# Relative products cut from eight to four at a place, value products to one block at a place, and the fourth unit's maxima folded earlier, in a two-layer attention kernel

## The chip, the cores and the metric

The kernel runs on one NeuronCore of a Trainium2 chip. The metric is the device time of one execution in microseconds (us). Three executions of the kernel before took 2415.1, 2431.35 and 2431.19 us; the median is 2431.19 us.

Names used here: PE is the matrix engine (TensorE), DVE the vector engine, ACT the scalar engine, POOL the GpSimd engine, and SP the sync engine, which here only issues transfers. PSUM is the memory that PE writes its products to.

## The reference

Eight images of 32 x 32 positions and 256 channels go through two layers. The first layer is a 3 x 3 convolution beside an attention of eight heads with relative position terms; the second is a plain attention and an expert network. What the change touches is the first layer's attention, cut here to its core:

```
kqv = einsum('bhwc,co->bhwo', x, qkv_w) + qkv_b           # k, q, v: 64 channels each
logits = einsum('bnid,bnjd->bnij', qf, kf)                # 1024 x 1024 for each head
rel_w = rel_logits_1d(qh, key_rel_w, H, W, ...)           # einsum of q with 63 relative keys,
rel_h = rel_logits_1d(qh_t, key_rel_h, W, H, ...)         # shifted to absolute positions
weights = softmax(logits + rel_w + rel_h, axis=-1)
attn = einsum('bnij,bnjd->bnid', weights, vf)
```

## The kernel before, in words

**Units and places.** The eight heads of an image form two groups of four (NG = 2), and the queries of a group form two halves of 512. A group and a half make a *unit*, so an image has four units. The tile `F` of a unit holds the query side of its logits on the partitions: the query itself, the two relative terms, and minus the row maximum. `KM` holds the key side. The logits of a unit are then single products of `KM` and `F`.

`first_layer(b)` walks over the four units of image `b`. Each unit has 32 *places* (eight key blocks times four heads), so an image has 128. At a place:

- `weigh` makes one product `st` (PE) and its exponential into `PT` (ACT);
- `score` makes products `lg` (PE) for the *next* unit and reduces each to a row maximum `mx` (DVE, line 782). A unit has 32 of them. The list `starts` says how many must be made by a given place;
- every fourth place `gather` multiplies `PT` with the values (`po`);
- when all 32 maxima stand, `fold` (place 25) combines them on DVE, `fold_in` (place 26) transposes them on PE (`pmx`) and copies them to `mb`, and `fold_out` (place 28) sends `mb` into the next unit's `F` by four small transfers issued on ACT (`F<-mb`, line 809);
- `fill.send` ends the place. It first runs what was put off to this place (`fill.later`), then lets the running chain go on to its next `yield None`, and then issues products of the convolution (`pc`) as far as the place's allowance of PE time is not used up.

After the first unit of an image, the whole second layer of the image before is worked off in one stretch of some 52 us.

**The chain of the next image.** `normalise(b + 1)` runs as such a chain during image `b`. From the first place of the third unit on it does, one step at a place: `queries` (transfers of the queries, lines 586 to 595), `values` (four blocks of products `pvv`, one block a place), three empty places, and then `features`. `features` makes the relative products: 32 for the columns and 32 for the rows, each a 128 x 64 product `prel`. A `piece` is eight of them in one PSUM tile of the pool that the `lg` tiles use too (four buffers). Four columns at four places, three rows at three places, two more places, the fourth row, three more places. A column's result goes through two copies on ACT (line 675) and two subtractions on DVE (line 676) into a float32r pair; a row's through one of each (lines 653 and 656). The subtractions run one place later, and a row's store into `fys` (line 661) one place after that. The four column stores into `fds` (line 682, 2 MB) follow the third row's stores in SP's queue.

Then `Unit(b + 1, 0)` is made. It issues six loads of its `F` on SP (lines 757 and 760, 2 MB). The buffer of this `F` is the one from which the rows are stored, so its first load waits until the last row store has landed. During the fourth unit of image `b` the maxima of this `Unit(b + 1, 0)` are made; the first `lg` product (place 5) needs the first three loads.

`combine(b + 1)` follows: four DVE operations, and, once the convolution of image `b` is done, ten more (line 534) at one a place.

**What sets the order.** The places write each engine's instructions in the order of the Python code; every engine works them off in that order. Transfers wait on SP, or on ACT, in the order of their issue.

Of the kernel before, what the change touches and what calls it, by code (L numbers as in the profile page):

```python
# [25 lines left out]
NG = NH // HG  # L26
# [12 lines left out]
def kernel(  # L39
# [72 lines left out]
    with ExitStack() as ph:  # L112
# [298 lines left out]
        def normalise(b):  # L411


            st = work.tile([P, KC, 2, 6], FP, tag="lst", name="gst")
            mv = work.tile([P, KC, 2], FP, tag="lmv", name="gmv")

            def turned(kc, g):
                tp = lg_tile("tpx")
                for k in range(4):
                    te.transpose(tp[:, k:512:4], T[b][g][:, k, kc * P : (kc + 1) * P], ident)  # L420
                return tp

# [24 lines left out]
            base = [b_tile("base") for kc in range(KC)]  # L447
            for g in range(2):
                for kc in range(KC):
                    nc.vector.tensor_scalar(  # L450
                        base[kc][:, g * 512 : g * 512 + 512],
                        turned(kc, g),
                        gm[:, kc, :],
                        gr[:, kc : kc + 1],
                        ALU.subtract,
                        ALU.mult,
                    )
                    yield None
            kq = b_tile("kq")
            kqh = work.tile([P, 2, S], FR, tag="kqh", name="kqh")  # L460
            kqb_ = kqh.bitcast(FP)

            for q in range(2):
                pk = lg_tile("pk")
                for kc in range(KC):
                    te.matmul(
                        pk,
                        lhsT=qkvw[:, kc, 0 : 2 * DK],
                        rhs=base[kc][:, 512 * q : 512 * (q + 1)],
                        start=kc == 0,  # L470
                        stop=kc == KC - 1,
                    )
                c = slice(q * 512, (q + 1) * 512)
                nc.scalar.activation(kq[:, c], pk, AF.Identity, bias=kqb, scale=kqs)
                nc.scalar.copy(kqh[:, 0, c], kq[:, c])
                nc.gpsimd.tensor_tensor(kqh[:, 1, c], kq[:, c], kqh[:, 0, c], ALU.subtract)
                yield None
            ready[b] = kqb_
            yield None
            while b > 0 and not may_query.get(b):  # L480
                yield None
            yield from queries(b)
            qs, qx, scr = spread.pop(b)
            if b > 0:
                keys(b, 0)
            for g in range(2):
                nc.gpsimd.tensor_tensor(T[b][g], T[b][g], l0b.to_broadcast([P, 4, C]), ALU.add)
            if b > 0:
                yield from values(b, base)
                for _ in range(3):  # L490
                    yield None
            yield from features(b, qs, qx, scr)
            units[b, 0] = Unit(b, 0)
            if b == 0:
                for g in range(NG):
                    keys(b, g, nc.scalar)
                yield None
                yield from values(b, base)
            while b > 0 and (done[b - 1] < 5 or not may_combine.get(b)):
                yield None  # L500
            yield from combine(b, base)
# [4 lines left out]
        def values(b, base):  # L506
            v0[b] = work.tile([P, NT, DK], FP, tag="v0", name="v0")
            for g in range(4):
                pv = lg_tile("pvv")[:, 0 : 2 * DK].rearrange("p (j c) -> p j c", c=DK)
                for j in range(2):  # L510
                    for kc in range(KC):
                        te.matmul(
                            pv[:, j, :],
                            lhsT=base[kc][:, (2 * g + j) * P : (2 * g + j + 1) * P],
                            rhs=qkvw[:, kc, 2 * DK : 3 * DK],
                            start=kc == 0,
                            stop=kc == KC - 1,
                        )
                nc.vector.tensor_tensor(
                    v0[b][:, 2 * g : 2 * g + 2], pv, vb.unsqueeze(1).to_broadcast([P, 2, DK]), ALU.add  # L520
                )
                yield None
# [104 lines left out]
        def features(b, qs, qx, scr):  # L627


            def piece(tab, src, q):  # L630
                pr = lg_tile("prel").rearrange("p (i g s) -> p i g s", g=NG, s=32)
                for n in range(8):
                    i = q * 8 + n
                    te.matmul(
                        pr[:, n],
                        lhsT=tab[:, (WW - 1 - i) * HG : (2 * WW - 1 - i) * HG],
                        rhs=src[:, :, i * 32 : (i + 1) * 32],
                        start=True,
                        stop=True,
                    )  # L640
                return pr
# [4 lines left out]
            ]  # L646

            def row(q):
                pr = piece(bhs, qs, q).rearrange("p i g s -> p g i s")
                r = b_tile("rel", FR) if q == 2 else scr[:, (2 + q % 2) * S : (3 + q % 2) * S]  # L650
                r = r.rearrange("p (l g s) -> p l g s", l=2, g=NG)
                hi, lo = (r[:, l].rearrange("p g (i s) -> p g i s", s=32) for l in range(2))
                nc.scalar.copy(hi, pr)

                def rest():
                    nc.vector.tensor_tensor(lo, pr, hi, ALU.subtract)
                    return store

                def store():
                    for g in range(NG):  # L660
# [2 lines left out]
                            in_=r.bitcast(FP)[:, :, g],  # L663
                        )

                fill.later(rest)

            def column(q):
                pr = piece(bws, qx, q)
                for g in range(NG):  # L670
                    ps = pr[:, :, g].rearrange("p x y -> p y x")
                    hi, lo = (
                        whole[g][:, l].rearrange("p (y x) -> p y x", x=WW)[:, :, q * 8 : q * 8 + 8] for l in range(2)
                    )
                    nc.scalar.copy(hi, ps)
                    fill.later(lambda ps=ps, hi=hi, lo=lo: nc.vector.tensor_tensor(lo, ps, hi, ALU.subtract) and None)
# [4 lines left out]
                    for p in (slice(HG, 64), slice(64, P)):  # L681
                        queue.dma_start(out=dst[p], in_=whole[g].bitcast(FP)[p])

            for q in range(4):
                column(q)
                yield None
            for q in range(3):
                row(q)
                yield None
                if b == 0 and q == 0:  # L690
                    store_columns(nc.scalar)
            yield None
            if b > 0:
                store_columns()
            yield None
            row(3)
            for _ in range(3):
                yield None

        done = {}  # L700
# [279 lines left out]
        def first_layer(b):  # L980


            more, sec = b + 1 < B, None
            starts = [lambda p: p * 4 // 3 + 1] * 3 + [lambda p: (p - 5) * 8 // 5 + 1]
            for s in range(NU * NT):
                n, j = divmod(s, NT)
                unit = units[b, n]
# [30 lines left out]
                for p in range(HG):  # L1018
                    place = 4 * j + p
                    unit.weigh(j, p)  # L1020
                    if nxt in units:
                        u = units[nxt]
                        while u.scored < min(32, starts[n](place)):
                            u.score()
                        if place == 25:
                            u.fold()
                        elif place == 26:
                            u.fold_in()
                        elif place == 28:
                            u.fold_out()  # L1030
                    elif nxt is not None:
                        assert place < 24
                    if p == 1:
                        if j > 0:
                            unit.gather()
# [489 lines left out]
```

## Time and profile before

The profiled execution took 2426.65 us; its span, from the first to the last instruction, is 2424.9 us.

| what | us |
|---|---|
| PE busy | 2203.9 (91% of the span) |
| DVE busy | 1384.1 (57%) |
| ACT busy | 1041.5 (43%) |
| POOL busy | 516.6 (21%) |
| `mx` reductions, 1024 | 657.8 |
| exponentials `PT`, 1024 | 596.9 |
| `st` products, 1024 | 519.2 |
| mean granted TensorE clock | 0.954 |

The first `st` runs at 124 us, the first layers end at 1858 us, and the expert network takes the rest. A table of the seven images in which the chain of the next image runs, from the trace's order of time (us from the start of the span; "third unit" is its first place, "column stores" the first issue of line 682, "F load" the first issue of line 757 after it, "first maximum product" the first `lg` of the next image, "next image" its first place):

| image | third unit | column stores | F load | first maximum product | next image |
|---|---|---|---|---|---|
| 0 | 204.2 | 230.7 | 243.5 | 251.5 | 282.4 |
| 1 | 422.1 | 450.0 | 462.2 | 478.6 | 509.8 |
| 2 | 654.8 | 681.8 | 694.3 | 703.0 | 733.6 |
| 3 | 875.1 | 907.2 | 920.1 | 930.9 | 961.4 |
| 4 | 1104.6 | 1138.6 | 1151.1 | 1163.3 | 1197.2 |
| 5 | 1338.8 | 1370.5 | 1383.8 | 1398.5 | 1429.0 |
| 6 | 1571.9 | 1605.7 | 1618.1 | 1630.7 | 1661.1 |

How to read it: the third unit takes 41 to 53 us although it holds the same work each time; and the last two columns are 30.4 to 33.9 us apart in every row.

### The profile page before, as it was taken

How to read it: one execution, taken by the hardware profiler on the slowest of the kernel's cores; microseconds unless marked ns; L12 is line 12 of the kernel's file. 1: busy time of each engine (PE TensorE's matmuls, PEld its weight loads, DVE VectorE, ACT ScalarE, POOL GpSimd, SP SyncE). 2: the span in 40 equal slices, each digit the busy share in tenths (PEclk: the TensorE clock that was granted, in tenths of full speed). 3: DMA queues.
4: the chain of work that ended last, by engine and by line, in shares of the span. 5: the costliest groups of instructions: out<-in, count | busy, mean ns of one | idle time of the engine just before them, and what ended most of it. 6: DMA issues, size and time to landing. Idle time of an engine off the chain costs nothing.

```text
span 2424.9 us, 28815 instructions
## 1 busy us (share of the span) xinstructions
PE 2203.9 (91%) x10515; PEld 1419.0 (59%) x10515; DVE 1384.1 (57%) x3147; ACT 1041.5 (43%) x1990; POOL 516.6 (21%) x446
## 2 busy tenths in 40 slices
PE   5589999899999999999899999999998789999998
PEld 4455556556555665566556556665664456666665
DVE  4667746575685666575657575657571633333333
ACT  2145544444454445444544454445454322222332
POOL 2213211320223022202120311131111042222220
PEclk7699999999999989998999899989998889999999
DMA  4634312701461245124312521361110121222210
GB/s 122 125 88 122 80 40 71 186 11 45 101 152 24 65 108 120 36 70 121 80 36 70 149 52 45 73 166 24 45 45 1 57 87 70 70 70 71 83 46 27
DMA packets 91935, 184.94 MB, mean 76 GB/s; under 512 B 9313, under 2 KB 37866, under 8 KB 90258
## 3 DMA queue, kind: packets, MB, share of 16 engines
q1 hardware_dynamic: 89426, 178.47, 29.2%
q10 hardware_dynamic: 2368, 4.63, 0.8%
q8 instruction: 84, 1.38, 0.2%
q14 instruction: 57, 0.47, 0.1%
HBM read 112.15 MB, written 62.52 MB: 72 GB/s over the span
## 4 chain that ended last, share of the span: by engine, by line
PE 64%; DVE 17%; DMA 7%; ACT 6%; SPq 3%; issue 2%; ACTq 1%; POOL 1%; DVEq 0%; POOLq 0%
PE po L133 11%; PE phd L1435 9%; PE py L1452 9%; PE lg L133 8%; PE st L133 8%; DVE mx L782 7%; PE pc L133 5%; PE pq L133 3%; PE prel L133 2%; DMA F<-mb 2%; ACT PT L826 2%; PE tp L137 2%; PE pa L133 1%; PE pv L133 1%; SPq L586 1%
## 5 line engine op out<-in xcount | busy, mean ns | idle before, releaser
L782 DVE TENSOR_REDUCE mx<-lg 128x1 f32<-128x512 f32 x1024 | 657.8, 686 | 255.7 <-PE lg L133 250.3
L826 ACT ACTIVATE PT<-st 128x512 f32<-128x512 f32 x1024 | 596.9, 598 | 445.2 <-PE st L133 396.3
L133 PE MATMUL st<-F,KM 128*128 128x512 f32 x1024 | 519.2, 512 | 36.1 <-ACT PT L826 23.0
L133 PE MATMUL lg<-KM,F 128*128 128x512 f32 x1024 | 393.6, 422 | 43.1 <-DMA F<-fy 34.6
L133 PEld LDWEIGHTS st<-F,KM 128*128 128x128 f32 x1024 | 198.9, 195 | 243.6 <-ACT PT L826 180.0
L133 PE MATMUL po<-PT,vk 128*32 128x512 f32 x2048 | 282.2, 620 | 0.0
L133 PE MATMUL pc<-convw,V 128*128 128x192 f32 x1152 | 269.7, 337 | 13.4 <-ACT mm L720 12.7
L133 PEld LDWEIGHTS lg<-KM,F 128*128 128x128 f32 x1024 | 200.5, 196 | 92.5 <-issue 39.2
L133 PEld LDWEIGHTS pc<-convw,V 128*128 128x128 f32 x1152 | 211.3, 195 | 60.6 <-issue 19.9
L1435 PE MATMUL phd<-n2T,w 128*128 128x512 f32 x512 | 226.9, 598 | 0.0
L1452 PE MATMUL py<-w,hT 128*128 128x256 f32 x1024 | 223.6, 379 | 0.0
L1452 PEld LDWEIGHTS py<-w,hT 128*128 128x128 f32 x1024 | 194.6, 190 | 33.3 <-issue 7.4
L1459 DVE TENSOR_TENSOR r<-py,n 128x256 f32<-128x256 f32 x64 | 27.2, 425 | 257.5 <-PE py L1452 257.5
L1435 PEld LDWEIGHTS phd<-n2T,w 128*128 128x128 f32 x512 | 96.3, 191 | 113.2 <-issue 109.3
L1065 DVE TENSOR_REDUCE nm<-lg 128x1 f32<-128x512 f32 x128 | 85.4, 686 | 113.2 <-PE lg L133 113.2
L1069 ACT ACTIVATE pr<-lg,nm 128x512 f32<-128x512 f32 x128 | 86.9, 683 | 126.5 <-DVE nm L1066 126.0
L1442 ACT ACTIVATE hT<-phd,b1c 128x512 f32<-128x512 f32 x128 | 86.4, 687 | 101.3 <-PE phd L1435 96.6
L133 PE MATMUL lg<-nqk 128*128 128x512 f32 x256 | 120.7, 594 | 0.0
L133 PE MATMUL po<-pt,v 128*128 128x256 f32 x512 | 115.8, 379 | 0.0
L730 POOL TENSOR_TENSOR ms<-mm 128x192 f32<-128x192 f32 x32 | 19.3, 603 | 446.7 <-ACT mm L720 446.5
L133 PEld LDWEIGHTS po<-pt,v 128*128 128x128 f32 x512 | 95.1, 190 | 11.6
L1390 POOL TENSOR_SCALAR w<-w,wbc 128x1024 f32<-128x1024 f32 x16 | 46.7, 2921 | 252.5 <-DMA w<-in_L_ffn_W_dram 167.8
(259 smaller groups left out, 2501.1 us busy)
## 6 DMA issues: line engine op xcount, KB each, us to landing
F<-fd SPq DMA_DIRECT2D x64, 768.0 KB
F<-fy SPq DMA_DIRECT2D x128, 128.0 KB
w<-in_L_ffn_W_dram SPq DMA_DIRECT2D x32, 512.0 KB
fy<-scr SPq DMA_DIRECT2D x48, 256.0 KB
T<-in_x_dram SPq DMA_DIRECT2D x16, 512.0 KB
fd<-kqh SPq DMA_DIRECT2D x32, 256.0 KB
Td<-T SPq DMA_DIRECT2D x16, 512.0 KB
T<-Td SPq DMA_DIRECT2D x8, 1024.0 KB
```

The costliest lines, as they stand in the source:

```text
L133: nc.tensor.matmul(out, **kw)
L137: nc.tensor.transpose(out, in_, ident)
L586: nc.sync.dma_start(out=qs.bitcast(FP)[32 * i : 32 * i + 32, g], in_=kqb_[DK + 32 * g : DK + 32 * g + 32, i // 2, :],)
L782: nc.vector.tensor_reduce(self.mx[:, a, i, hl : hl + 1], lg, AX.X, ALU.max, negate=True)
L826: nc.scalar.activation(self.pts[j][:, hl, :], st, AF.Exp)
L1065: nc.vector.tensor_reduce(nm[:, h : h + 1], lg[h], AX.X, ALU.max, negate=True)
L1069: nc.scalar.activation(pr[:, h * 512 : (h + 1) * 512], lg[h], AF.Exp, bias=nm[:, 2:3], scale=scale, accum_out=rs[:, h, i : i + 1],)
L1390: nc.gpsimd.tensor_scalar(w2t, w2t, wbc[:, n : n + 1], None, ALU.mult)
L1435: nc.tensor.matmul(phd, lhsT=ws[k][0][:, kc, f * P : (f + 1) * P], rhs=n2T[:, kc, q * 512 : (q + 1) * 512], start=kc == 0, stop=kc == KC - 1,)
L1442: nc.scalar.activation(hT[:, k * NF + f, :], phd, AF.Gelu, bias=b1c[:, f, k * B + b : k * B + b + 1])
L1452: nc.tensor.matmul(py, lhsT=hT[:, k * NF + f, j * P : (j + 1) * P], rhs=ws[k][1][:, f, :], start=k + f == 0, stop=k == TOPK - 1 and f == N ...
L1459: nc.vector.tensor_tensor(r[:, j, :], py, n2[:, q * 4 + j, :], ALU.add)
```

## The change

Four edits, all in the part above:

- `values` ends a place after every block of 128 positions, so its eight half steps take eight places; the three empty places behind it go.
- a `piece` makes four relative products in place of eight. The columns take eight places, and a row two (`row` now yields between its halves); two places behind the rows go. Each half has its own copies and subtractions; a row's store is still one, after its second half.
- `starts`: the maxima of the fourth unit, made during the third, go at three for two places in place of four for three; those of the next image's first unit, made during the fourth, begin at place 6 in place of 5 and go at sixteen for nine places in place of eight for five.
- the fourth unit's maxima are folded at place 22 in place of 25, transposed at 23, and sent at 25.

```diff
             if b > 0:
                 yield from values(b, base)
-                for _ in range(3):
-                    yield None
             yield from features(b, qs, qx, scr)
...
                             stop=kc == KC - 1,
                         )
+                    if j == 0 and b > 0:
+                        yield None
...
             def piece(tab, src, q):
-                pr = lg_tile("prel").rearrange("p (i g s) -> p i g s", g=NG, s=32)
-                for n in range(8):
-                    i = q * 8 + n
+                pr = lg_tile("prel")[:, 0:256].rearrange("p (i g s) -> p i g s", g=NG, s=32)
+                for n in range(4):
+                    i = q * 4 + n
...
-                fill.later(rest)
+                for h in range(2):
+                    pr = piece(bhs, qs, 2 * q + h).rearrange("p i g s -> p g i s")
+                    hi, lo = (
+                        r[:, l, :, h * 128 : h * 128 + 128].rearrange("p g (i s) -> p g i s", s=32) for l in range(2)
+                    )
+                    nc.scalar.copy(hi, pr)
+
+                    def rest(pr=pr, hi=hi, lo=lo, h=h):
+                        nc.vector.tensor_tensor(lo, pr, hi, ALU.subtract)
+                        return store if h else None
+
+                    fill.later(rest)
+                    yield None
...
-            for q in range(4):
+            for q in range(8):
                 column(q)
                 yield None
             for q in range(3):
-                row(q)
-                yield None
+                yield from row(q)
                 if b == 0 and q == 0:
                     store_columns(nc.scalar)
             yield None
             if b > 0:
                 store_columns()
-            yield None
-            row(3)
-            for _ in range(3):
+            yield from row(3)
+            for _ in range(2):
                 yield None
...
-            starts = [lambda p: p * 4 // 3 + 1] * 3 + [lambda p: (p - 5) * 8 // 5 + 1]
+            starts = [lambda p: p * 4 // 3 + 1] * 2 + [lambda p: p * 3 // 2 + 1, lambda p: (p - 6) * 16 // 9 + 1]
+            folds = (25, 25, 22, 25)
...
-                        if place == 25:
+                        if place == folds[n]:
                             u.fold()
-                        elif place == 26:
+                        elif place == folds[n] + 1:
                             u.fold_in()
-                        elif place == 28:
+                        elif place == folds[n] + 3:
                             u.fold_out()
```

More of the change, by code (lines that the diff above doesn't have):

```diff
@@ L648, in row @@
             def row(q):
-                pr = piece(bhs, qs, q).rearrange("p i g s -> p g i s")
                 r = b_tile("rel", FR) if q == 2 else scr[:, (2 + q % 2) * S : (3 + q % 2) * S]
                 r = r.rearrange("p (l g s) -> p l g s", l=2, g=NG)
[L652 to L657, printed above, removed]
                 def store():
@@ L672, in column @@
                     hi, lo = (
-                        whole[g][:, l].rearrange("p (y x) -> p y x", x=WW)[:, :, q * 8 : q * 8 + 8] for l in range(2)
+                        whole[g][:, l].rearrange("p (y x) -> p y x", x=WW)[:, :, q * 4 : q * 4 + 4] for l in range(2)
                     )
@@ L1024, in first_layer @@
                             u.score()
-                        if place == 25:
+                        if place == folds[n]:
                             u.fold()
-                        elif place == 26:
+                        elif place == folds[n] + 1:
                             u.fold_in()
-                        elif place == 28:
+                        elif place == folds[n] + 3:
                             u.fold_out()
                     elif nxt is not None:
-                        assert place < 24
+                        assert place < folds[n] - 1
                     if p == 1:
```

## The prediction

> **What bounds the kernel now.** I read first the page's shares and slices, for where PE is full and at which clock.
>
> ```profile
> PE 2203.9 (91%) x10515; PEld 1419.0 (59%) x10515; DVE 1384.1 (57%) x3147; ACT 1041.5 (43%) x1990; POOL 516.6 (21%) x446
> ...
> PEclk7699999999999989998999899989998889999999
> ```
>
> PE is the bound of the whole, but its clock dips once an image from the fourth on. Second, the stretches of the third units (start and length, then busy us of PE, weight loads, DVE, ACT, POOL, then granted clock, DMA share and GB/s), for images 2 and 4, and image 4's cut into four:
>
> ```profile
> 654.80:697.20 42.40, 40.94 (x254) 27.27 (x253) 31.62 (x60) 23.51 (x48) 17.74 (x18) 1.00 0.69 180
> ...
> 1104.60:1157.70 53.10, 48.95 (x259) 34.54 (x258) 31.67 (x59) 24.07 (x47) 20.49 (x21) 0.84 0.60 156
> ```
>
> ```profile
> 1104.60:1118.20 13.60, 13.60 (x94) 10.41 (x92) 8.86 (x17) 5.36 (x10) 7.75 (x4) 1.00 0.96 217
> 1118.20:1121.60 3.40, 1.84 (x15) 0.70 (x13) 1.42 (x4) 2.15 (x6) 0.70 (x1) 1.00 0.36 63
> 1121.60:1138.70 17.10, 17.10 (x63) 13.53 (x63) 9.19 (x18) 6.88 (x15) 0.97 (x2) 0.50 0.18 63
> ```
>
> The same work takes 42.4 us at full clock and 53.1 where PE, after 1.56 us of idleness, ran 17.1 us at half clock through the relative products. Images 3 to 6 show this (clock 0.84 to 0.86), images 0 to 2 not. Third, the order of time of SP's queue and PE in image 0, for what the next image's first unit waits for:
>
> ```profile
> 230.71 5.27 SPq L682 DMA_DIRECT2D fd<-rel  x4
> 236.07 4.25 SPq L661 DMA_DIRECT2D fy<-scr  x2
> 243.51 0.60 SPq L757 DMA_DIRECT2D F<-fd  x1
> ```
>
> ```profile
> 251.51 0.47 PE L133 MATMUL lg<-KM,F 128*128 128x512 f32 x1 [0.67 <-DMA F<-fy]
> ```
>
> From the first column store to the load of `F` are 12.8 us (12.2 to 13.3 in all seven images, at either clock), and from there 8.0 us until the first maximum product can run. So `F` is ready 20.5 us after the column stores begin, and in image 0 PE waited for it already. Fourth, what follows that product is DVE's:
>
> ```profile
> 1163.70:1187.50 23.80, 22.97 (x115) 12.06 (x114) 23.16 (x42) 12.47 (x22) 1.58 (x2) 1.00 0.48 91
> ```
>
> DVE is busy 23.16 of 23.80 us from the first maximum to the last. That is why first maximum product and next image are 30.4 to 31.2 us apart in six of seven rows of the table. What decides an image's time is thus the distance from its third unit to the first maximum product: 47.3, 56.5, 48.2, 55.8, 58.7, 59.7, 58.8 us, 385.0 in all.
>
> **The change, part by part.** *The longer product stretch.* The last product of the third row was at place 13 and is now at place 21. Before it PE must issue, in addition, eight `st` at 0.31 us from start to start, fourteen `lg` at 0.24 (18 by place 13, 32 by place 21), two gathers at 1.0 and one `pc` at 0.16: 2.5 + 3.4 + 2.0 + 0.2 = 8.1 us. The products themselves cost the same 0.10 us each, 64 an image. Behind the last product the store had to wait 2.5 us (1135.2 to 1137.7: `st`, `lg`, a 0.60 reduction, a 0.60 subtraction); now no `lg` lies between, a cast of 0.38 and a subtraction of 0.34 remain, some 1.3: minus 1.2. DVE has no reserve in the stretch: four places hold six reductions at 0.60 and eight subtractions of 128 elements, which I estimate at 0.21 (0.60 for 512 elements and 0.34 for 256 give 0.001 an element), 5.3 us, and PE in them 4 x 0.31 + 6 x 0.24 + 1.0 + 16 x 0.10 = 5.3. Two engines that feed each other through four buffers lose something: plus 0.9, between 0 and 3. The column stores began at 26.5, 27.9 and 27.0 us where the clock was full, 27.1 on average; they now begin at 27.1 + 8.1 - 1.2 + 0.9 = 34.9. Twelve casts and twelve subtractions an image become 24 each: ACT gains 1.6 us of work beside 24 busy of 42, hidden.
>
> *What is late next.* `F` is ready at 34.9 + 20.5 = 55.4 us. PE would be there earlier: 42.4 us for a third unit, 5.8 to the old place 5 in image 2 (697.2 to 703.0) and 0.9 for a place more make 49.1. So PE waits about 6 us for the load, in every image, with `st`, `gather` and the convolution queued behind that `lg`, and ACT and DVE behind them. Seven times 55.4 is 387.8, against 385.0: **plus 2.8 us**. The clock's gain in images 3 to 6 and the loss in 0 and 2 cancel.
>
> *The clock behind that wait.* A wait of 2.55 us (466.2 to 469.6, PE busy 0.85 of 3.40) was followed by 3.4 us at half clock. At half clock a place of the fourth unit with 1.78 `lg` takes PE some 1.8 us (0.57 for `st`, 0.43 for `lg`, a quarter of 1.9), while DVE asks for 1.07 to 1.6. Over two places DVE starves 0.5 to 1.5 us; I take 1.3 for seven images: **plus 9**. Bounds 0 and 20.
>
> *The earlier fold.* `st` waited for `F<-mb` 12.8 us in eight times. This wait goes or stays without effect: whatever PE wins at place 0 it loses at place 6, where the load decides. Nor is it sure to go: the four transfers took 6.1 us behind their last issue beside the loads of `F` (image 2), 1.65 alone, and now run beside the column stores.
>
> *The value products* spread over eight places: same count, and the first column moves one place back. ACT's first column cast waited until 15.3 us after the unit's start for the query transfers (1119.45, 3.47 us idle) and still will; PE's wait behind it shrinks from 1.55 to some 0.7. In the sum above.
>
> *The new pace.* Place 6 in place of 5: the same 32 reductions and seven of the ten line 534 operations lie behind the first product, so 23.8 us stay. *Image 0's own features and image 7* (no features; its third unit takes 30.7 us with DVE busy 21.9): 0, between -1 and +2.
>
> Sum against the profiled execution: 2426.65 + 2.8 + 9 = **2438 us**. The median of the three runs, 2431.19, lies 4.5 above the profiled execution; I leave the sum where it is.
>
> A rule to weigh: the Trainium skill (TensorE: Matmul & The Clock Gate, "Why this matters for your kernels") asks for no idle gap of PE over some 3 us. The trace is stricter: 1.56 us of idleness among the small products was enough. By the page the third units of both kernels would keep the clock and only the 6 us wait would close it. The sum by it would be the same; the second rival below would cost nothing.
>
> **Rivals.** *Faster: the load is not late.* If the column stores begin at 29.5, because the places with four products run into time that PE and ACT lost before, the first product comes at 50.0: 350 against 385.0, minus 35, **2392 us**. For it: PE idles 1.5 us in image 2's third unit, and the clock stays. Against it: 8.1 us of PE work stand before the store, and DVE is as full as PE. Half way, at 32, it is 2411 with half the clock's loss.
>
> *Slower: the clock closes inside the longer stretch.* At half clock a place costs 0.57 + 1.5 x 0.43 + 4 x 0.21 + 0.25 x 1.9 = 2.5 us against 1.3; from place 10 to 21 that is 12 x 1.2 = 14 us an image, and the load moves with it. In the old stretch half clock lasted as long as the products did, and now they last twice as many places. [...] For it: four of seven images before. [...] Three images make 2438 + 42 = **2480 us**.
>
> *The change does not do what it says.* The built order has four products at each of the places 8 to 21, 23 and 24, and the fold at 22; only the fold's gain can fail, and it is not in the sum.
>
> **How the numbers follow.** Measured change under 1% (24 us) can hardly be told from none. Forecast 0.54, centre 2438, own range 2415 to 2460 (the bounds 0 and 3 of DVE's loss and 0 and 20 of the clock's, not all at one end, and an us either way in the 8.1). Faster 0.12. Slower 0.34, from two images (2466) to four (2494). Leaving out the outer half of each rival gives 2400 to 2484.
>
> **What would show it.** Third units at clock 1.00 and 41 to 43 us; column stores at 33 to 36 us after the unit's start; `lg` waiting 3 to 7 us for `F<-fy` at place 6 of each fourth unit, with half clock behind it. Column stores before 31 us, or no such wait, prove the second step wrong and make the kernel faster; a third unit with clock under 0.9 proves the rival.

## The result, and the profile after

The changed kernel takes 2440.06 us (median of nine executions, 2434.04 to 2450.48), the kernel before 2420.92 beside it (nine, 2413.42 to 2431.35; the three executions named at the start are the first of them): ratio 1.0082, 95% interval 1.0054 to 1.011. That is under 1%, as forecast, and on the slower side. The profiled execution took 2441.9 us with a span of 2440.1: 15.2 more than the span of before. The page's shares and clock:

```profile
PE 2191.9 (90%) x10515; PEld 1400.4 (57%) x10515; DVE 1384.3 (57%) x3243; ACT 1050.7 (43%) x2086; POOL 510.2 (21%) x446
...
PEclk7698999999999999999999999999999989999999
```

PE is busy 12 us less than before and the clock's dips of images 3 to 6 no longer show in the slices, yet the span is longer: PE waits more. The third units of images 2 and 4 of the changed kernel, as stretches (start and length, then busy us of PE, weight loads, DVE, ACT, POOL, then granted clock, DMA share and GB/s):

```profile
674.60:724.40 49.80, 45.75 (x265) 30.25 (x264) 31.98 (x70) 25.09 (x59) 20.38 (x21) 0.93 0.57 148
1133.60:1182.50 48.90, 44.42 (x262) 29.27 (x262) 31.54 (x70) 24.96 (x59) 20.34 (x21) 0.97 0.59 150
```

Image 4's clock rose from 0.84 to 0.97, but its unit is still 48.9 us long, 6.5 more than image 2 of before at full clock: PE idles 4.5 us in it in place of 1.5, and is busy for 44.4 in place of 40.9. The busy part is longer because 3.4 us run at half clock, and because the unit does not hold the same work each time: it takes convolution products `pc` by the allowance of its places, 31 here and 23 in image 2 of before. What holds PE is seen in image 3. The order of time of SP's queue, then of ACT, then of PE (start, length, what; in brackets the idle time before it and what ended it), all of the changed kernel:

```profile
939.89 5.27 SPq L687 DMA_DIRECT2D fd<-rel  x4
945.26 4.15 SPq L654 DMA_DIRECT2D fy<-scr  x2
953.18 0.59 SPq L760 DMA_DIRECT2D F<-fd  x1
```

```profile
941.75 0.60 ACT L829 ACTIVATE PT<-st 128x512 f32<-128x512 f32 x1 [0.46 <-PE st L133]
941.81 5.34 ACTq L812 DMA_DIRECT2D F<-mb  x4
947.20 1.09 ACT L829 ACTIVATE PT<-st 128x512 f32<-128x512 f32 x2 [4.86 <-issue]
```

```profile
947.85 0.61 PE L133 MATMUL st<-F,KM 128*128 128x512 f32 x1 [3.83 <-ACT PT L829]
...
961.01 0.47 PE L133 MATMUL lg<-KM,F 128*128 128x512 f32 x1 [1.15 <-DMA F<-fy]
```

The column stores begin at 939.9, 35.2 us after the unit's start; the load follows 13.3 us later and the first maximum product 7.8 after that. This is the forecast's chain. Not forecast is the second view: while SP issues the stores, ACT needs 5.34 us to *issue* the four small `F<-mb`, its exponentials stand behind them, and PE waits 3.83 us for them before the `st` of place 28. With that, little of its waiting is left for place 6. DVE's stretch from the first maximum to the last is as full as before:

```profile
961.50:984.30 22.80, 21.61 (x104) 11.36 (x103) 22.71 (x39) 11.24 (x19) 0.77 (x1) 1.00 0.57 118
```

The seven images, from the order of time, in us. "u3" is the third unit's length; the next columns count from its start; "PE waits" are PE's waits behind ACT before the `st` of place 28 (the gaps that the expectations put at places 25 to 27) and for `F<-fy` at place 6 of the fourth unit.

| image | u3 before | u3 after | half clock in it, after | column stores, after | F load, after | first maximum product, before | after | PE waits, after |
|---|---|---|---|---|---|---|---|---|
| 0 | 41.4 | 52.9 | 17.1 | 41.6 | 54.7 | 47.3 | 62.6 | 3.65, 4.54 |
| 1 | 47.2 | 50.3 | 6.8 | 37.1 | 50.9 | 56.5 | 59.0 | 3.26, 3.02 |
| 2 | 42.4 | 49.8 | 6.8 | 35.2 | 48.5 | 48.2 | 57.1 | 3.37, 1.45 |
| 3 | 48.5 | 49.3 | 3.4 | 35.2 | 48.5 | 55.8 | 56.4 | 3.83, 1.15 |
| 4 | 53.2 | 48.9 | 3.4 | 34.7 | 48.0 | 58.7 | 55.5 | 3.91, 0.71 |
| 5 | 49.1 | 46.1 | 0 | 35.0 | 47.5 | 59.7 | 55.5 | 2.62, 3.48 |
| 6 | 52.9 | 49.0 | 3.4 | 35.0 | 48.1 | 58.8 | 56.2 | 3.75, 1.34 |
| sum | 334.6 | 346.5 | | | | 385.0 | 402.3 | 24.4, 15.7 |

So the span's 15.2 us are: 17.3 from the third units' starts to the first maximum products, 1.4 from there to the next image (218.0 and 219.4), 3.0 up to image 0's third unit, minus 6.4 in the stretches from an image's start to its third unit (987.0 and 980.6), and nothing behind the last of them. The parts add up to 15.3 with their rounding.

### The profile page after: what moved, and what is told of

The parts are those of the page before. It is cut to its first block, busy times and chain, and to the rows that moved or that the text cites. A ratio compares the mean times of both kernels' runs of the same rounds, so it can differ in the third digit from the quotient of the medians.

```text
span 2440.1 us, 29073 instructions
## 1 busy us (share of the span) xinstructions
PE 2191.9 (90%) x10515; PEld 1400.4 (57%) x10515; DVE 1384.3 (57%) x3243; ACT 1050.7 (43%) x2086; POOL 510.2 (21%) x446
## 4 chain that ended last, share of the span: by engine, by line
PE 63%; DVE 17%; ACT 5%; DMA 5%; issue 4%; ACTq 2%; SPq 2%; POOL 1%; DVEq 0%; POOLq 0%
PE po L133 10%; PE phd L1439 9%; PE py L1456 9%; PE lg L133 8%; DVE mx L785 8%; PE st L133 7%; PE pc L133 5%; PE pq L133 2%; ACTq L812 2%; DMA F<-fy 2%; PE prel L133 2%; PE tp L137 2%; ACT PT L829 2%; PE pa L133 1%; PE pv L133 1%
## 5 line engine op out<-in xcount | busy, mean ns | idle before, releaser
L133 PE MATMUL st<-F,KM 128*128 128x512 f32 x1024 | 514.1, 508 | 42.1 <-ACT PT L829 41.9
L133 PE MATMUL pc<-convw,V 128*128 128x192 f32 x1152 | 265.8, 338 | 18.9 <-ACT mm L723 18.5
```

Source lines behind the costliest of these rows:

```text
L133: nc.tensor.matmul(out, **kw)
```

## The experiments

The theory at the start was that of the prediction: an image's time is set by when the next image's `F` can be loaded. The rivals were PE and its clock, and the wait that the profile after had shown, ACT's issuing. Each kernel was compared with the kernel before on the same chip; ratios are to it, with 95% intervals. The two kernels with the fourth edit and POOL on the kernel before, the fourth edit alone and the row stored twice have four executions each, the others nine or ten. "Distance" is the sum of the seven stretches from third unit to first maximum product, from one profiled execution (before 385.0, changed 402.3). Which images meet half clock differs between kernels and between two profiles of one kernel, and a distance holds that too.

| kernel | median us | ratio | interval | distance |
|---|---|---|---|---|
| changed | 2440.06 | 1.0082 | 1.0054 to 1.011 | 402.3 |
| changed, without the fourth edit | 2436.19 | 1.0067 | 1.0035 to 1.0099 | 393.9 |
| changed, old values | 2435.82 | 1.0078 | 1.0041 to 1.0116 | 403.2 |
| changed, early column stores | 2415.6 | 0.9988 | 0.9955 to 1.0021 | 379.7 |
| changed, `F<-mb` on POOL | 2412.93 | 0.9966 | 0.9939 to 0.9993 | 395.3 |
| changed, two places later | 2427.69 | 1.003 | 0.9994 to 1.0066 | 406.2 |
| changed, fourth row stored twice | 2466.57 | 1.021 | 1.0129 to 1.0291 | 413.9 |
| before, early column stores | 2440.65 | 1.0096 | 1.0062 to 1.013 | 399.5 |
| before, fourth edit alone | 2385.83 | 0.9848 | 0.9771 to 0.9924 | 355.9 |
| before, faster maxima alone | 2400.72 | 0.9939 | 0.9909 to 0.997 | 361.6 |
| before, fourth edit, `F<-mb` on POOL | 2398.29 | 0.9898 | 0.9819 to 0.9978 | 384.1 |
| before, fourth edit, POOL for all but the fourth unit's | 2374.05 | 0.9816 | 0.9738 to 0.9894 | 353.0 |

### The fourth edit undone in the changed kernel

```diff
-            starts = [lambda p: p * 4 // 3 + 1] * 2 + [lambda p: p * 3 // 2 + 1, lambda p: (p - 6) * 16 // 9 + 1]
-            folds = (25, 25, 22, 25)
+            starts = [lambda p: p * 4 // 3 + 1] * 3 + [lambda p: (p - 6) * 16 // 9 + 1]
+            folds = (25, 25, 25, 25)
```

> The changed kernel without its fourth edit: the fourth unit's maxima again four for three places, folded at place 25 and sent at 28. Theory (load of F): the stall of ACT at places 25 to 27 of the third unit (24.4 us of PE gaps) goes or moves to place 28 to 31, PE's wait for F<-mb at the fourth unit's start comes back in part, but the column stores stay at 35 us and the load decides, so the time is within 8 us of 2440. Rival (the stall at place 25 is on the path): 12 to 24 us go, 2416 to 2428.

Measured 1.0067 against 1.0082, intervals that overlap. PE's wait behind the stall of ACT went to the `st` of place 31 (3.5 to 4.4 us; the four issues took 4.6 to 6.5 us there), since at place 28 the column stores and, behind them, the fourth row's are still being issued. In this kernel's profile no stretch of relative products fell to half clock, and its distance is 8.4 less, but its time is not. In the changed kernel the fourth edit is worth nothing that can be measured, as both the forecast and the theory had it.

### The fourth edit alone in the kernel before

```diff
-            starts = [lambda p: p * 4 // 3 + 1] * 3 + [lambda p: (p - 5) * 8 // 5 + 1]
+            starts = [lambda p: p * 4 // 3 + 1] * 2 + [lambda p: p * 3 // 2 + 1, lambda p: (p - 5) * 8 // 5 + 1]
+            folds = (25, 25, 22, 25)
```

(with the three places of the fold taken from `folds`, as in the change)

> The kernel before with the fourth edit alone: the fourth unit's maxima at three for two places, folded at 22, sent at 25. Theory (load of F): the waits for F<-mb at the fourth unit's start (12.8 us) go, and as much is waited for the load at place 5 wherever the load is late; where the half clock made PE later than the load, some of it is won: 0 to 10 us faster. Rival (the early sending collides with the column stores on the issuing engines): ACT's four issues take 4 to 5 us in place of 2.1 in most images and the time is 10 to 20 us longer.

Measured 0.9848, some 34 us less in the medians: more than either expectation allowed. What PE waited for, from the view of waits (us in total, times, longest), in the order before, changed, this kernel:

```profile
PE st L133 <- ACT PT L826: 23.0, 39, 1.0
...
PE st L133 <- DMA F<-mb: 12.8, 8, 2.5
```

```profile
PE lg L133 <- DMA F<-fy: 43.9, 8, 26.7
PE st L133 <- ACT PT L829: 41.9, 37, 3.9
```

```profile
PE lg L133 <- DMA F<-fy: 33.5, 3, 28.6
PE st L133 <- ACT PT L826: 29.3, 42, 2.0
```

In both kernels with the sooner fold the wait for `F<-mb` is off the list (of the waits for `F<-fy`, one of 26.7 and of 28.6 us lies ahead of the first image). In the changed kernel 18.9 us come back as waits for ACT (41.9 against 23.0); here 6.3 do, because the four `F<-mb` come at or behind the last of the column stores' issues (2.4 to 3.4 us for four). The distance falls by 29.1: the stretches from the fourth unit's start to the first maximum product lose 20.6 (50.4 to 29.8), more than the 12.8 of the wait, and the third units 8.5. Their clock, images 2 and 4 of this kernel:

```profile
650.40:694.60 44.20, 42.42 (x263) 28.31 (x261) 32.54 (x60) 23.73 (x47) 20.84 (x20) 1.00 0.69 180
1094.00:1141.70 47.70, 45.74 (x262) 30.43 (x260) 32.53 (x60) 23.73 (x48) 20.80 (x20) 0.93 0.64 168
```

Image 4 has 0.93 where before had 0.84, with the old eight products a place. `F` loads at 39.7 to 44.5 us after the unit's start, and the first maximum product comes 8.1 to 10.7 later, at 48.7 to 52.7. So the other edits, put on top of this one, cost some 54 us (2386 to 2440), 46.4 of them in the distance: they move the load by 7.7 us an image (from 41.8 on average to 49.5) to where it decides.

### The faster maxima alone in the kernel before

```diff
-            starts = [lambda p: p * 4 // 3 + 1] * 3 + [lambda p: (p - 5) * 8 // 5 + 1]
+            starts = [lambda p: p * 4 // 3 + 1] * 2 + [lambda p: p * 3 // 2 + 1, lambda p: (p - 5) * 8 // 5 + 1]
```

> The kernel before with one line alone: the fourth unit's maxima at three for two places in place of four for three; they are folded and sent where they were, at places 25 and 28. It parts what the fourth edit gave alone (2386, 34 less than before): the third units' lengths fell by 8.5 us in seven images and the stretch from the fourth unit's start to the first maximum product by 20.6. Theory (the sooner sending gave most: the waits for F<-mb and the half clock behind them in the fourth unit): 2405 to 2420, third units 3 to 10 us shorter in all, waits for F<-mb still there. Rival (more long products among the short ones keep the clock, and that gave all): 2392 or less, third units at full clock.

Measured 0.9939, 2400.72, between the two expectations. The profile shows more of the rival than I had allowed: six of the seven third units are at full clock and they lost 29.4 us together (334.6 to 305.2). But 6.0 of it came back behind them (50.4 to 56.4), where the waits for `F<-mb` remain (10.8 us), each with 3.4 us or more of half clock behind it in four images. So the fourth edit seems to have two halves, the clock of the third unit and the wait at the fourth's start. This half alone takes 23.4 us off the distance, both take 29.1; the load at 40 to 45 us, ready 8 us later, leaves no room for much more. That the long maximum products among the short ones keep the clock is not shown. With the same pace, the relative products met half clock in one image of seven here, in three with the fourth edit alone, and in five and three of its two versions with POOL below; in the kernel before it was four. The time of this kernel is firmer than its share of clock.

### The values as before

```diff
                 yield from values(b, base)
+                for _ in range(3):
+                    yield None
             yield from features(b, qs, qx, scr)
...
-                    if j == 0 and b > 0:
-                        yield None
```

> The changed kernel with the values as before: two blocks of products a place at four places, then three empty places, so that the first column comes one place sooner; four relative products a place and the fourth edit stay. Theory (load of F): column stores 1.3 us sooner, at 33.6 to 34, and 7 to 10 us go: 2430 to 2435. Rival (the value products, spread over eight places, keep PE's clock or DVE's pace in the first places): third units with more half clock and the time at 2440 or above. Rival (the products in small pieces cost nothing and the values cost all): 2400 or less.

Measured 1.0078, not to be told from 1.0082. The column stores came at 34.3 to 36.3 us in six images, hardly sooner, and at 39.3 in image 5 behind half clock. The first column came only 0.8 us sooner, and ACT's first cast of it no sooner at all (14.0 to 15.6 us after the unit's start, 14.2 to 15.1 in the changed kernel). So of the 54 us the value products hold nothing measurable; by elimination it is the small pieces, the maxima's start at place 6 and what comes with them. No run parts these from each other.

### Column stores sent sooner, in the changed kernel and in the kernel before

```diff
-                if b == 0 and q == 0:
-                    store_columns(nc.scalar)
+                if q == 0:
+                    store_columns(nc.scalar if b == 0 else nc.sync)
             yield None
-            if b > 0:
-                store_columns()
```

> The changed kernel with the four column stores of 2 MB sent right behind the first row, some eight places sooner, and nothing else changed. Theory (the time is set by when the next image's F can be loaded: column stores, 13.2 us to the load, 8.0 us to the first maximum product, 31 us to the next image): the load is then held only by the last row's store, at place 27 to 28 of the third unit (39 to 41 us after its start in place of 48), F is ready at 47 to 49 us, PE's wait for F<-fy at place 6 of the fourth unit is gone, the first maximum product comes at 49 to 51 us after the third unit's start in place of 55.5 to 62.6 (402.4 in seven images), and 40 to 55 us go: 2385 to 2400. Rival (PE is the bound and its wait only moves; or DVE): the first maximum product stays at 55 or later for another reason and the time is within 8 us of 2440. Rival (ACT held while it issues the four F<-mb at place 25 beside the column stores): the 3 to 4 us gaps of PE at places 25 to 27, 24 us in all, go with the collision, and at least half of the gain is read there and not at place 6.

> The kernel before with its column stores sent right behind the first row, some six places sooner, and nothing else changed. Theory (load of F): F is ready at 35 to 40 us after the third unit's start and no longer decides; the first maximum product comes when PE gets to place 5 of the fourth unit: 47 to 48 us in images whose third unit keeps the full clock, 53 to 59 in those with the half clock, 385 in seven images becomes 360 to 375, and 10 to 25 us go (about 2400). If the early stores also keep the clock open, 48 x 7 = 336 and 2375. Rival (the distance is set by PE and its clock alone, the load is always hidden): within 5 us of before.

The changed kernel won 24 us (0.9988), less than the 40 to 55 expected: the load came at 44.1 to 47.5 us after the unit's start, where 39 to 41 had been expected, and the distance fell by 22.6. The kernel before *lost* 21 us (1.0096), against all that was expected. Its order of time on SP and ACT, image 3:

```profile
917.20 5.76 SPq L661 DMA_DIRECT2D fy<-scr  x4
923.08 1.25 SPq L661 DMA_DIRECT2D fy<-rel  x2
927.16 1.09 SPq L661 DMA_DIRECT2D fy<-scr  x2
```

```profile
925.83 0.58 ACT L653 CAST scr<-prel 128x512 fp32r<-128x512 f32 x1 [6.95 <-DMA fy<-scr]
```

The rows' stores now stand in SP's queue behind the 2 MB, and their issues, 0.44 us each in the old place, take 1.44. The fourth row is written to the buffer of the second, so its cast waits for that store to land: ACT stood 6.95 us, its exponentials behind the cast, and PE 5.0 us before the `st` of place 19. That is so in images 0 and 3. In the other five ACT's wait before that cast is some 1.5 us: there 13.7 to 17.1 us of half clock in the relative products had made the cast itself late. The distance grew by 14.5 in the profile: by 19.3 in images 0 to 2, of which 1 and 2 had no half clock in the kernel before, and minus 4.8 in images 3 to 6. So the wait for the store explains a part of the loss; why images 1 and 2 met half clock is open. In the changed kernel with the sooner stores the same wait of ACT is in all seven images (3.8 to 4.6 us). In these two kernels a store sent sooner paid only as far as no later one that something waits for stood behind it.

### `F<-mb` issued on POOL

```diff
-                    nc.scalar.dma_start(
+                    nc.gpsimd.dma_start(
                         out=self.Fb[R_M : R_M + 33 : 32, :, h],
```

> The changed kernel with the four small transfers F<-mb of every unit issued on POOL in place of ACT. Theory (the load of F decides in the changed kernel; the stall of ACT at places 25 to 27 only takes PE's waiting away from place 6): ACT's exponentials are no longer held, the seven gaps of 2.6 to 3.9 us at places 25 to 27 of the third units go, PE's wait for F<-fy at place 6 of the fourth unit grows by about as much (15.7 us in seven images become 30 to 40), the first maximum product stays at 55 to 56 us, and the time is 2428 to 2442. Rival (the stall of ACT is what the changed kernel lost): 20 us or more go, 2420 or less. Rival (POOL, busy 20 of 49 us with the key copies, sends late): waits for F<-mb at the fourth unit's start come back, 12 us or more, and the time is above 2445.

> The kernel before with the fourth edit alone, and the four F<-mb of every unit issued on POOL. There the stall of ACT (issues of 2.4 to 3.4 us in place of 2.1, PE gaps of 1 to 2 us at places 26 and 27) stands where PE and not the load is last in most images. Theory: these gaps, some 10 us in seven images, go and 5 to 10 us with them: 2376 to 2381. Rival (the load is already last at 48 to 52 us): within 4 us of 2386. Rival (POOL sends late): 10 us or more above it.

In the changed kernel 27 us went (2412.93, ratio 0.9966). The theory's 2428 to 2442 was missed: the time is that of the first rival, and the waits for `F<-mb` are those of the second. ACT's stall is gone, as the waits show:

```profile
PE st L133 <- DMA F<-mb: 26.3, 7, 4.6
...
PE st L133 <- ACT PT L829: 11.1, 20, 0.7
```

But the distance fell by only 7.0: POOL, between its convolution work, sent the four at 41.6 to 45.4 us after the unit's start in images 1 to 6, in place of 36.7 to 39.0, and there PE waits 3.9 to 4.6 us for `F<-mb` before the fourth unit's first `st`. The wait moved again; most of what else was won (the profile's span is 32.9 us shorter) lies outside the distance, in all units: first maximum product to next image 209.2 in place of 219.4, an image's start to its third unit 965.8 in place of 980.6, where ACT no longer issues 128 transfers at 0.52. That these issues are the cause there is argued, not shown. The same edit on the kernel before with the fourth edit lost 12 us in the medians, with intervals that overlap, as its last expectation had it: there POOL's late sending brought back the waits (19.3 us), five stretches of relative products met half clock in place of three, and the distance grew by 28 us, against 22 us won elsewhere.

The next one takes the good half of both:

```diff
-            def fold_out(self):
+            def fold_out(self, queue=nc.gpsimd):
...
-                            u.fold_out()
+                            u.fold_out(nc.scalar if n == 2 else nc.gpsimd)
```

> The kernel before with the fourth edit alone, the F<-mb of the fourth unit issued on ACT as there, those of all other units on POOL. With all of them on POOL the stretches from the first maximum product to the next third unit took 1176.6 us in seven images in place of 1198.3, and the third units with the start of the fourth lost 28 because POOL sent the fourth unit's late. Theory (both add up): the first maximum products stay at 356 us in seven images and some 20 us go elsewhere: 2362 to 2372. Rival (the fourth unit loses on POOL whatever is done, or the clock takes it back): 2380 or more.

Measured 2374.05, ratio 0.9816 (0.9738 to 0.9894): faster than the kernel before and the changed one. It is 2 us above what was expected. The distance stayed (353.0), the rest fell by 14.5 (1198.3 to 1183.8), less than the 20 added up. Its interval overlaps that of the fourth edit alone (0.9771 to 0.9924), so the gain from POOL beside that edit is not shown by the times.

### What follows the column stores, two places later

```diff
             if b > 0:
+                yield None
+                yield None
                 store_columns()
             yield from row(3)
```

> The changed kernel with the column stores and the fourth row, and all that follows them, two places later. Theory (load of F, slope one): everything from the column stores to the first maximum product comes 2.6 to 3.2 us later in each of seven images, 58 to 59 us after the third unit's start, PE's wait at place 6 grows by that, and the time is 2458 to 2465. Rival (the load has slack, PE's own work sets the 55.5 us): within 6 us of 2440.

The expectation failed, and so did the edit: the stores stayed at 35 us and the load at 48 to 49 us in images 2 to 6. SP does not go by places. It issues what stands in its queue as soon as the data are there, and the column stores follow the third row's stores in any case; only the fourth row moved. Its stores were issued 2.1 to 3.8 us later in images 2 to 6, but two issues took 1.5 to 2.4 us together in place of 3.6 to 4.5, and the load came 0.5 us later on average. So it says little on the slope. That the time fell a little (1.003, its interval overlapping that of the changed kernel) came from the stretches between an image's start and its third unit (969.6 against 980.6); why is open.

### The load made later without touching PE, DVE or ACT

```diff
                 def store():
-                    for g in range(NG):
+                    for g in range(NG) if q < 3 or b == 0 else (0, 1, 0, 1):
```

> The changed kernel with the fourth row's two stores issued twice (the same data to the same place), so that the load of F, which waits for them, starts later and nothing on PE, DVE or ACT changes. Each issue behind the 2 MB took 1.7 to 2.4 us, so the load should start 2.5 to 4 us later. Theory (the load sets the first maximum product once it is later than PE; PE waited 0.7 to 4.5 us for it): nearly all of that is paid, 2 to 4 us in each of seven images, and half clock behind it: 2455 to 2472. Rival (the load has slack and PE's own work sets the 55 us): within 6 us of 2440.

Measured 2466.57, ratio 1.021: 26.5 us more than the changed kernel. SP's queue in image 3:

```profile
941.57 5.23 SPq L687 DMA_DIRECT2D fd<-rel  x4
946.89 7.87 SPq L654 DMA_DIRECT2D fy<-scr  x4
957.11 0.60 SPq L760 DMA_DIRECT2D F<-fd  x1
```

From the first column store to the load are 15.5 us in place of 13.3. In images 3 to 6 the load came 2.0 to 2.8 us later, the first maximum product 1.9 to 2.7 later, and PE's waits for `F<-fy` went from 1.2, 0.7, 3.5 and 1.3 to 4.4, 3.6, 3.5 and 6.3. In the changed kernel the load decides, with a slope near one: the theory holds where it was meant to hold. From there to the next image are 4.7 more (219.4 to 224.1), with half clock behind the longer wait in every image. The rest of the profile's 21.9 us is no part of the theory: beside 11.7 in the distance and these 4.7 there are 2.9 between an image's start and its third unit, 3.7 behind the last third unit's start and minus 1.0 ahead of the first.

### The changed kernel itself once more

> The changed kernel itself once more, for a second profile. The first has 17.1 us of half clock in image 0's third unit and its first maximum product 62.6 us after that unit's start, against 55.5 to 59.0 in the other images. If that belongs to the kernel, it is there again and the seven distances add up to 400 to 405 us; if it falls on one execution and not on another, image 0 comes to 57 to 59 and the sum to 393 to 400, with the time within 10 us of 2440 in both cases.

It took 2443.04 us and the seven distances add up to 402.2 again, but the long images are others, so that neither half of the expectation came as it was put: image 0 has 55.9 us, image 1 62.3, image 2 59.2. The window of image 1 cut into three (columns as above):

```profile
432.70:447.60 14.90, 14.90 (x96) 9.92 (x95) 10.32 (x20) 5.99 (x11) 8.15 (x4) 1.00 0.90 202
447.60:450.20 2.60, 1.35 (x9) 0.98 (x9) 1.97 (x6) 2.46 (x9) 0.37 (x1) 1.00 0.40 57
450.20:467.30 17.10, 17.10 (x70) 11.50 (x69) 10.11 (x26) 7.38 (x21) 0.00 (x0) 0.60 0.01 1
```

PE idled 1.25 us while the second piece waited for the first one's subtraction, and 13.7 of the next 17.1 us ran at half clock. So in both profiles one image has 13.7 us of half clock in the product stretch and the next image 3.4; which image it is changes.

## Why the prediction came out as it did

**The longer product stretch** (column stores at 34.9): 35.0 on average in images 3 to 6, and 34.7 to 35.2 in five images of the second profile. Right as a sum; its 0.9 for two engines that feed each other was chosen between 0 and 3, and no run shows it alone. The exception is the half clock below.

**What is late next** (first maximum product at 55.4 in every image, sum 387.8, plus 2.8). The mechanism held, and the doubled store shows its slope. The sum was mis-sized: 402.3, so plus 17.3. Images 3 to 6 give 56.4, 55.5, 55.5 and 56.2, on average 0.5 above 55.4. From the stores to the first product they have 20.9 us; the forecast went on with 20.5, where its own lines (12.8 and 8.0) give 20.8. Of the 14.5 us too much, 12.5 are in images 0 to 2: 7.2 and 3.6 in images 0 and 1, where the products fell into half clock and the stores came at 41.6 and 37.1, and 1.7 in image 2, whose stores came in time, at 35.2, and whose product ran 8.6 us behind the load in place of 7.5 to 8.1.

**PE would be there at 49.1 and wait 6 us.** This step failed. It took 42.4 us for a third unit; the units took 46 to 50 at nearly full clock. The sum had no term for ACT, whose issues of `F<-mb` make PE wait 2.6 to 3.9 us, nor for the 3.4 us or more of half clock that follow in six images, nor for the convolution products that a longer unit takes in (31 to 33 in images 2 to 6, where the 42.4 us held 23). PE got to place 6 at 52 to 58 us and waited 2.2 us on average. The end did not move, because the load came at its time all the same.

**The clock behind that wait** (plus 9, bounds 0 and 20): 1.4 from first maximum product to next image. The wait was shorter than forecast and only three images had half clock in the fourth unit (4.3 to 6.8 us). Where the wait was 3.5 to 6.3 us, with the store doubled, 6.1 were lost: still below nine, within its bounds.

**The earlier fold** (nothing, because the load takes back what PE wins): right for the changed kernel, 1.0067 without and 1.0082 with it. Its reason was right too, that four transfers beside the column stores would suffer, but it was thought of as their landing; what suffered was their issuing, and through it ACT. In the kernel before, where the load was ready in time, the same edit is worth 34 us. The forecast never priced it there; that a gain is buried by another edit can only be seen when each is priced alone.

**The clock's rule.** The forecast read from image 4 that 1.56 us of idleness among the small products was enough to lose the clock. The same profile says less: image 1 idled 1.59 us at that place and kept full clock, images 3 and 5 lost it behind 0.95 and 0.96. The length of one gap does not decide in that kernel.

**The rivals.** *The clock closes inside the longer stretch* happened in part, in one image for 13.7 us and in the next for 3.4, in place of three for the whole stretch; it was priced at 14 us an image, and the images with 13.7 us lost 6 to 7. With the two errors of the other sign, the clock behind the wait (minus 7.6) and the stretches that were counted as zero (3.0 and minus 6.4), the time came out within 2 us of the forecast. Part of that closeness is luck: two misses of 14.5 and minus 7.6 in the terms cancel by half. And the forecast started from the profiled execution, 2426.65, 5.7 above the median beside the result: the change itself was forecast as 11.8 us and measured as 19.1 in the medians (15.2 in the profiles). *The load is not late*: no, only with the stores sent sooner (its half-way price should read 2414 and not 2411: 7 x 52.5 is 17.5 less than 385.0, and half the clock's loss 4.5 more). *The change does not do what it says*: it does, and the half of it that pays is lost in the rest.

## What to carry to other kernels

Price each edit of a change alone, on the kernel before: here one was worth 34 us and the others hid it by moving a transfer by 7.7 us an image to where it was last. A transfer issued on ACT cost ACT the time of its issue, and beside SP's large stores that was not the time it has alone (up to 5.3 us for four in place of 2.1); look for what is in flight at the new place. SP, which only issues, went by data and order and not by the places of the program, so the edit that put the column stores "later" in the code did not move them, and the one that put them sooner slowed the stores right behind them.

## What the runs showed of the hardware

**Issues behind large stores.** One `F<-mb` takes 0.52 us to issue on ACT (median of 128), four 2.1. Beside the four column stores they took 4.0 to 5.3 us in the changed kernel (up to 2.23 for one), 4.6 to 6.5 without the fourth edit, and 2.1 again where the column stores had been sent sooner. The two row stores right behind the 2 MB on SP took 1.8 to 2.4 each (mean of the two), against some 0.44 ahead of them. What holds the issues is not shown. POOL's were not held: 2.27 us for four, while SP needed 4.41 for its two. The changed kernel with `F<-mb` on POOL, SP's order and POOL's, image 3:

```profile
926.34 4.41 SPq L654 DMA_DIRECT2D fy<-scr  x2
```

```profile
928.24 2.27 POOL L812 DMA_DIRECT2D F<-mb  x4
```

The Trainium skill (DMA: Bandwidth & Descriptors, "Issuing engines are not separate DMA queues") says that issuing on several engines saves only the issuing time, "which is usually small relative to the DMA itself". These runs show an exception: that time grew from 2.1 to as much as 6.5 us for four, and it stood on the path of an engine with other work.

**Half clock after short idleness, and without it.** In all versions with four products a place, take the place where the second small piece waits for the first one's subtraction. In twelve images PE idled 1.10 to 1.91 us there, and in ten of them 3.4 to 13.7 us of half clock followed within 3 us; the two others had 1.10 and 1.24. In all other images it idled up to 0.93 us, and never ran at half clock in the stretch behind it. With eight products a place no such line can be drawn: beside the images of the kernel before named above, 6.8 to 13.7 us of half clock began 17.6 to 20.7 us after the unit's start in twelve images of the four kernels that put the faster maxima on it, and in eleven of these PE had not idled over 0.5 us at a time since the first relative product. What else decides is open. Behind the stall of ACT before the `st` of place 28, 3.4 us or more of half clock came in six of seven images in both profiles of the changed kernel; the seventh, image 5, had the shortest stall (2.62 and 2.47 us).
